# Layer 0 of a four-layer network: one more fold of the bias rows by DMA, another order of the fold's steps on GpSimd, eleven row buffers, and query and value weights of one pair at a time

## The chip, the cores and the metric

The program runs on one core of a Trainium2 chip. The metric is the device time of one execution in microseconds; the kernel before took 3342.97 us (median of three runs, 3342.06 to 3345.39). The engines are TensorE (PE: matmuls; PEld: its weight loads), VectorE (DVE), ScalarE (ACT), GpSimd (POOL) and SyncE (SP, which here only issues DMAs).

## What is computed

Four layers follow each other on an input of 2 x 512 x 32 x 32; only layer 0 is changed. It is a deformable attention with a bias that is computed by a small network. Cut to what matters:

```python
pos  = grid_q[:, :, None, :] - grid_kv[:, None, :, :]   # 1024 queries x 64 keys x 2
bias = sign(pos) * log1p(abs(pos))
bias = relu(bias @ cpb_w1 + cpb_b1)                     # 2 -> 128
bias = relu(bias @ cpb_w2 + cpb_b2)                     # 128 -> 128
bias = bias @ cpb_w3 + cpb_b3                           # 128 -> 1
sim  = einsum('bhid,bhjd->bhij', qh, kh) + bias         # scores
out  = softmax(sim) @ vh
```

There are 2 images and 8 heads, so 16 (image, head) pairs of 1024 queries by 64 keys, and the 2 -> 128 -> 128 -> 1 network is evaluated for each of these million combinations. All of it is in 32-bit floats. Layers 1 to 3 (attention with group norm) and the feed-forward part of layer 0 follow; they are not touched.

## The kernel before, in words

**Tiles and steps.** Two heads make a pair, and a tile is one image and one pair: 8 tiles (`NT`), each of 128 keys on partitions by 1024 queries. The bias of a tile is computed in 32 steps (`NR`) of four keys each; the loop of 256 steps is in `layer0`.

**One step.** `first` (L604, VectorE) adds a row table and a column table and clips at zero: the hidden layer of 128 units for two keys, 1024 queries. Two calls serve a step; they run eight keys ahead, in a ring of six buffers. `second` (L621, PE) multiplies by the 128 x 128 matrix in four parts of 32 units each; in each part the four keys fill the four blocks of 32 partitions of one PSUM tile. ScalarE applies bias and relu (L630) into an SBUF buffer of 128 partitions (4 keys x 32 units) by 1024 queries, 512 KB. The four parts come in the order 1, 0, 3, 2. Parts 1 and 3 go to a pool of four buffers, part 2 to a pool of three, part 0 to a buffer that lives longer.

**Joining and folding.** The last product, 128 -> 1, is a sum over units with signs that were pulled out beforehand. VectorE adds part 1 to part 0 and part 3 to part 2 (`joined`, L635). The rest of the sum over units is done on transfers that add to their destination, which only GpSimd issues:

- the join (L939, 512 KB): the part 2 buffer is added to the part 0 buffer of the same step;
- the first fold (L932, 256 KB): odd partitions are added to even ones;
- the second fold: partitions 2 of 4 are added to partitions 0 of 4 (128 KB), which leaves 32 of the 128 partitions. For the first step of each group of four it is done in place (L934). For the other three, SyncE copies their rows into the group's first buffer (L936, a plain copy) and GpSimd adds the other half there (L942).

So one buffer holds the rows of four steps. `third` (L650, PE) multiplies four such buffers by a matrix of zeros and signs (`w3_16`), four abreast, each 128 x 32 by 512 columns, for two halves of the queries, and so adds 16 steps to `sim` in PSUM. A matmul of this size in 32-bit floats stands in the trace as two records. A tile takes two such calls, 20 steps after the first step of each half. The last 16 steps of the last tile use a shorter form (L921 to L927, L971, and `finish_last`).

**Buffers.** The buffers of group-first steps go round in a ring of six, those of the other steps in a ring of four. Eight of these ten are 4 KB slots per partition of a tile named `bridge` that also carries weights before and sums after the loop.

**Around it.** After the second call of a tile, `scores` adds query times key to `sim`, and a chain of small pieces named `behind` is started: `finish` (softmax and the product with the values), `offsets` of the tile after next, `samples` of the next tile. One piece runs at every odd quarter of a step (k = 1 and 3), so the small work lies spread between the matmuls. `scale_tab` (L592) scales the tables for each four steps on ScalarE, in steps 1 mod 4; SyncE loads them (L573) in steps 2 mod 4.

**What sets the order.** Every engine runs its instructions in the order in which the program text issues them, and each queue, GpSimd's and SyncE's among them, waits in that order: an instruction that waits holds up all behind it. Within a step i and quarter k, before, GpSimd gets: at k = 0 the first fold of step i-2; at k = 1 the join of step i-1, then the second fold of step i-3; at k = 3, for a group's first step only, the second fold of step i-2. SyncE gets the copy of step i-2 at k = 3.

**Weights of layer 0's projections.** Query and value weights stand in block-diagonal form for all four pairs (`bd`, `vwbd`, `qws`); `offsets` uses `qws` of one pair, `samples` the value weights of one pair.

Of the kernel before, what the change touches and what calls it, by code (L numbers as in the profile page):

```python
# [12 lines left out]
F32 = mybir.dt.float32  # L13
# [66 lines left out]
def kernel(ctx: ExitStack, tc: tile.TileContext, a: dict, out: bass.AP):  # L80
# [111 lines left out]
    def layer0(l0, fold_d, t2_b, o2_b):  # L192
# [7 lines left out]
        h2p = cycle([bridge[:, k, :] for k in range(6)])  # L200
        h2j = cycle([bridge[:, 6, :], bridge[:, 7, :], *(one.tile([P, HW], F32, name=f"h2j{k}") for k in range(2))])
# [18 lines left out]
        qkw = next(h2j).rearrange("p (j q n) -> p j q n", j=2, q=NPAIR)  # L220
        vw = one.tile([P, NPAIR, P], F32, name="vwbd")
        bd = {"qw": qkw[:, 0], "kw": qkw[:, 1], "vw": vw}
# [21 lines left out]
        def late_loads():  # L244
            load_groups("vw")
            nc.sync.dma_start(out=xs[1], in_=a["x"][1].rearrange("(k p) n -> p k n", p=P))
# [7 lines left out]
        qws = one.tile([P, NPAIR, P], F32, name="qws")  # L254
        nc.vector.tensor_scalar(qws[:, 0, :], bd["qw"][:, 0, :], s1[:, 0:1], None, ALU.mult)
# [21 lines left out]
        w3_16 = one.tile([P, 48], F32, name="w3_16")  # L277
# [7 lines left out]
        def bias_weights():  # L285
# [5 lines left out]
            few = one.tile([P, 28], F32, name="few")  # L291
# [69 lines left out]
            quarter = few[:, 26:28]  # L361
            for k in range(2):
                nc.vector.tensor_reduce(quarter[:, k : k + 1], ident[:, 2 + k : P : 4], AX.X, ALU.add)
                nc.vector.scalar_tensor_tensor(eighth, quarter[:, k : k + 1], 8.0, eighth, ALU.mult, ALU.add)
            nc.vector.tensor_scalar(w3_16[:, 16:32], row[:, 0:16], eighth, 0.0, ALU.add, ALU.is_equal)
            nc.vector.tensor_scalar(w3_16[:, 16:32], w3_16[:, 16:32], w3sign[:, 1:2], None, ALU.mult)
# [15 lines left out]
        def offsets(t):  # L382
# [4 lines left out]
            for half in range(2):  # L387
                n = slice(half * HALF, (half + 1) * HALF)
                nc.tensor.matmul(pq[:, n], qws[:, pr, :], xs[b][:, pr, n], start=True, stop=True)
# [60 lines left out]
            pos = two.tile([P, 2, 32], F32, name="pos")  # L450
# [14 lines left out]
            sgn = two.tile([P, 2, 32], F32, name="sgn")  # L465
# [19 lines left out]
        def samples(t):  # L485
# [5 lines left out]

            gp = gps.pop(t)
# [7 lines left out]
            near = two.tile([P, 2, 32], F32, name="near")  # L500
            wsum = two.tile([P, 3], F32, name="wsum")
            for ax in range(2):
                nc.scalar.activation(near[:, ax, :], ir, AF.Abs, bias=gp[:, ax : ax + 1], scale=-1.0)
                nc.scalar.activation(
                    near[:, ax, :], near[:, ax, :], AF.Relu, bias=1.0, scale=-1.0, accum_out=wsum[:, ax : ax + 1]
                )
            nc.vector.tensor_mul(wsum[:, 2:3], wsum[:, 0:1], wsum[:, 1:2])
# [33 lines left out]
            nc.tensor.matmul(pkv[:, 1, :], bd["vw"][:, pr, :], kv, start=True, stop=True)  # L541
# [17 lines left out]
        NCH = NR // 4  # L559
        LAST = NT * NR - 16  # L560
        tabs_of = {}

        def load_tabs(c):

            t, rc = divmod(c, NCH)
            assert t in tables
            tabs_of[c] = []
            for ax in range(2):
                src = slog_d[t, ax].rearrange("(q r) i -> q r i", q=4)
                tab = (one if ax else two).tile([P, 16, 32], F32, name=f"tab{ax}")  # L570
                if 4 * c < LAST:
                    q, r = rc % 4, rc // 4 * 16
                    nc.sync.dma_start(out=tab, in_=src[q, r : r + 16, :].partition_broadcast(P))  # L573
                else:
                    q, r = rc % 2 * 2, 16 + (rc - 4) // 2 * 8
                    nc.sync.dma_start(
                        out=tab.rearrange("p (q r) i -> p q r i", q=2),
                        in_=src[q : q + 2, r : r + 8, :].partition_broadcast(P),
                    )
                tabs_of[c].append(tab)  # L580
# [33 lines left out]
        def second(i, h1s, part):  # L614

            z = zt([P, HW], "z")
            lo = BLOCK[part]
            for half in range(2):
                n = slice(half * HALF, (half + 1) * HALF)
                for point in range(4):  # L620
                    nc.tensor.matmul(  # L621
                        z[point * 32 : point * 32 + 32, n],
                        cpb_w2[:, lo : lo + 32],
                        h1s[point][:, half * 16 : half * 16 + 16, :],
                        start=True,
                        stop=True,
                    )
            ring = h2q if part % 2 else h2b if part else h2j if i % (4 if i < LAST else 2) else h2p
            h2 = ring.tile([P, HW], F32, name="h2", tag="h2") if ring in (h2q, h2b) else next(ring)
            nc.scalar.activation(h2, z, AF.Relu, bias=b2h[:, part : part + 1])  # L630
            return h2
# [8 lines left out]
        def third(sim, r, h2s, fours=(), halves=range(2), wide=False):  # L640

            for half in halves:
                n = slice(half * HALF, (half + 1) * HALF)
                w = w3_16[:, 16 - r : 48 - r] if wide else w3[:, 24 - r : 56 - r]
                ways = [(quad, w, h2) for quad, h2 in enumerate(h2s)]
                for k in range(2):
                    w = w3_4[:, 28 - r - 4 * k : 60 - r - 4 * k]
                    ways += [(quad, w, pair[k]) for quad, pair in enumerate(fours, len(h2s))]
                for k, (quad, w, h2) in enumerate(ways):
                    nc.tensor.matmul(  # L650
                        sim[quad * 32 : quad * 32 + 32, n], w, h2[:, n], start=(r == 0 and k < 4), stop=False
                    )
# [9 lines left out]
        def finish(t, sim):  # L662

            b, pr = divmod(t, NPAIR)
            if pr == 0:
                aTs[b] = one.tile([P, NPAIR, HW], F32, name="aT")
            simb = one.tile([P, HW], F32, name="simb", tag="wy")
# [22 lines left out]
            nc.vector.tensor_tensor(atv, atv, sm.unsqueeze(2).to_broadcast([P, 16, NJ]), ALU.mult)  # L690
            yield
# [96 lines left out]
        def key_weights():  # L788
# [26 lines left out]
        nc.vector.tensor_tensor(  # L815
            qws[:, 1:], bd["qw"][:, 1:], s1[:, 1:].unsqueeze(2).to_broadcast([P, NPAIR - 1, P]), ALU.mult
        )
# [3 lines left out]
        nat = [[next(h2p).rearrange("p (k n) -> p k n", k=2) for _ in range(2)] for _ in range(3)]  # L821
# [68 lines left out]
        h1s, parts, joins, sim, w1s = {}, {}, {}, None, None  # L890
        behind = chain(small_steps, offsets(1), samples(0))
# [5 lines left out]
        for i in range(steps):  # L897
            for k, part in enumerate((1, 0, 3, 2)):
# [5 lines left out]
                due = i - 20  # L904
                if k == 1 and 0 <= due < LAST and due % 16 == 0:
                    t, r = divmod(due, NR)
                    if r == 0:
                        sim = ps_s.tile([P, HW], F32, name="sim")
                    third(sim, r, [joins.pop(due + j) for j in range(0, 16, 4)], wide=True)
                    if r:  # L910
                        assert next(behind, None) is None
                        scores(t, sim)
                        behind = chain(
                            finish(t, sim),
                            offsets(t + 2) if t + 2 < NT else iter(()),
                            samples(t + 1) if t + 1 < NT else iter(()),
                        )
# [3 lines left out]
                if LAST <= i - 2 and i < steps - 2:  # L921
# [4 lines left out]
                    if i - 3 >= LAST and i % 2 and k == 3:  # L926
                        nc.gpsimd.dma_start(out=joins[i - 3][1:P:2], in_=joins.pop(i - 2)[1:P:2], accum_op=ALU.add)  # L927
                if 0 <= i - 2 < LAST:
                    j = (i - 2) % 4
                    whole, own = joins[i - 2 - j], joins[i - 2]  # L930
                    if k == 0:
                        nc.gpsimd.dma_start(out=own[0:P:2], in_=own[1:P:2], accum_op=ALU.add)  # L932
                    if k == 3 and j == 0:
                        nc.gpsimd.dma_start(out=own[0:P:4], in_=own[2:P:4], accum_op=ALU.add)  # L934
                    if k == 3 and j:
                        nc.sync.dma_start(out=whole[j:P:4], in_=own[0:P:4])  # L936
# [3 lines left out]
                j = (i - 3) % 4  # L940
                if k == 1 and 0 <= i - 3 < LAST and j:
                    nc.gpsimd.dma_start(  # L942
                        out=joins[i - 3 - j][j:P:4], in_=joins.pop(i - 3)[2:P:4], accum_op=ALU.add
                    )
# [5 lines left out]
                if k == 1 and due == LAST:  # L950
                    third(sim, 16, [joins.pop(due + j) for j in range(0, 8, 2)])
# [1325 lines left out]
```

## Time and profile before

The runs took 3342.97, 3345.39 and 3342.06 us. The profiled execution took 3343.91 us; its span, from the first to the last instruction, is 3342.0 us.

| what | before |
|---|---|
| time of the profiled execution | 3343.91 us |
| its span | 3342.0 us |
| PE busy | 3319.8 us (99%) |
| VectorE busy | 2640.9 us (79%) |
| ScalarE busy | 1809.4 us (54%) |
| GpSimd busy | 675.3 us (20%) |
| loop of layer 0 (first z matmul to the last join's landing) | 57 to 1975 us |
| records of L621 (z) | 16384, 0.59 us each, four abreast |
| records of L650 (sim) | 280 |
| DMA engines busy in the loop | 78 to 79% |

In the profile, a group's line gives the source line, the engine, the operation, the tiles written and read, the count, the busy time and the mean duration in ns, and after the bar the idle time of the engine just ahead of it with what ended that idle time. In a timeline the columns are start and duration in us, engine, line, operation, tiles, and in brackets the idle time before it and what ended it. In a line of the waits stand the engine that waited, for what, and the total in us, the number of waits and the longest. A line of the windows gives the stretch, its length, the busy times of PE, PEld, DVE, ACT and POOL with their counts, the granted clock, the busy share of the DMA engines and GB/s.

### The profile page before, as it was taken

Reading aid. Unit: us, or ns where it says so; the run is one execution under the profiler, and the core shown is the slowest. Engines: PE = TensorE matmul, PEld = TensorE weight load, DVE = VectorE, ACT = ScalarE, POOL = GpSimd, SP = SyncE. Lnnn points to the kernel's source line nnn. Section 1 sums busy time; section 2 is a strip of 40 time slices with the busy share of each in tenths; the row PEclk is TensorE's granted clock in tenths of the full one; section 3 lists DMA queues with packets and bytes.
Section 4 is the critical chain, followed back from the end, with each engine's and each line's share of the span. In section 5 each row is a group of like instructions: output and inputs, shape, how many; then the busy total and the mean of one; then the engine's idle time right before and its main releaser. Section 6 shows DMA issues by size and latency. Waiting matters only on the chain.

```text
span 3342.0 us, 60958 instructions
## 1 busy us (share of the span) xinstructions
PE 3319.8 (99%) x24813; PEld 1605.2 (48%) x24813; DVE 2640.9 (79%) x3029; ACT 1809.4 (54%) x2774; POOL 675.3 (20%) x803
## 2 busy tenths in 40 slices
PE   9999999999999999999999999999999999999999
PEld 4333333333333333333333339999953443687777
DVE  6999999999998799999999966455446465765556
ACT  4866877877876677877867642112126245122221
POOL 1333333333333233333333210000000000000000
PEclk9999999999999999999999999999999999999999
DMA  5777877787787577778877741000100000000111
GB/s 171 158 162 161 162 164 156 158 169 152 160 166 158 107 165 151 161 165 160 166 159 152 161 120 58 14 9 12 51 0 14 26 32 17 7 7 4 29 33 36
DMA packets 142482, 343.91 MB, mean 103 GB/s; under 512 B 36465, under 2 KB 51441, under 8 KB 141425
## 3 DMA queue, kind: packets, MB, share of 16 engines
q0 software_dynamic: 68400, 231.26, 37.1%
q1 hardware_dynamic: 72496, 103.95, 10.1%
q8 instruction: 197, 3.23, 0.4%
q10 hardware_dynamic: 1296, 4.72, 0.4%
q14 instruction: 93, 0.75, 0.1%
HBM read 71.46 MB, written 10.83 MB: 25 GB/s over the span
## 4 chain that ended last, share of the span: by engine, by line
PE 96%; DVE 1%; issue 1%; ACT 1%; DMA 1%; SPq 0%; POOL 0%; DVEq 0%; ACTq 0%; POOLq 0%
PE z L621 52%; PE pma L135 6%; PE pw L1440 6%; PE pmb L135 5%; PE pmv L1440 4%; PE score L1619 3%; PE pv L1631 3%; PE pm L1440 3%; PE score L1440 3%; PE ppr L1440 1%; PE pmt L1440 1%; PE sim L650 1%; PE pf L135 1%; PE pp L710 1%; PE pma L1343 1%
## 5 line engine op out<-in xcount | busy, mean ns | idle before, releaser
L621 PE MATMUL z<-wa,cpb_w 128*32 128x512 f32 x10880 | 1191.9, 593 | 2.7 <-ACT h L630 2.7
L630 ACT ACTIVATE h<-z,b2h 128x1024 f32<-128x1024 f32 x768 | 851.1, 1113 | 331.0 <-PE z L621 301.7
L604 DVE CUSTOM_DVE_ANT_1 wa<-tab,pairs 128x2048 f32<-128x2048 f32 x340 | 776.4, 2284 | 3.1 <-PE z L621 2.6
L621 PEld LDWEIGHTS z<-wa,cpb_w 128*32 128x32 f32 x10880 | 346.5, 110 | 809.3 <-issue 712.4
L621 PE MATMUL z<-h,cpb_w 128*32 128x512 f32 x5504 | 609.5, 593 | 0.7 <-ACT h L630 0.7
L604 DVE CUSTOM_DVE_ANT_1 h<-tab,pairs 128x2048 f32<-128x2048 f32 x172 | 392.7, 2284 | 1.7 <-PE z L621 1.5
L621 PEld LDWEIGHTS z<-h,cpb_w 128*32 128x32 f32 x5504 | 175.1, 110 | 407.9 <-issue 362.7
L635 DVE SCALAR_TENSOR_TENSOR h<-h,turn,h 128x1024 f32<-128x1024 f32 x256 | 327.1, 1278 | 5.5 <-ACT h L630 5.5
L630 ACT ACTIVATE bridge<-z,b2h 128x1024 f32<-128x1024 f32 x162 | 180.8, 1116 | 119.0 <-PE z L621 119.0
L932 POOL DMA_DIRECT2D bridge<-bridge x150 | 127.5, 850 | 539.5 <-DMA bridge<-h 517.5
L635 DVE SCALAR_TENSOR_TENSOR bridge<-bridge,turn,h 128x1024 f32<-128x1024 f32 x162 | 207.0, 1278 | 4.3 <-ACT bridge L630 4.3
L939 POOL DMA_DIRECT2D bridge<-h x161 | 158.4, 984 | 247.0 <-DVE h L635 151.8
L1283 ACT COPY p<-pma 128x128 f32<-128x128 f32 x80 | 21.3, 266 | 334.7 <-PE pma L135 334.7
L1275 DVE TENSOR_TENSOR upper<-pma,p 128x256 f32<-128x256 f32 x80 | 33.7, 421 | 178.6 <-ACT p L1283 178.5
L1620 ACT ACTIVATE p<-score 128x512 f32<-128x512 f32 x256 | 130.0, 624 | 81.2 <-PE score L1619 79.4
L932 POOL DMA_DIRECT2D h2j<-h2j x90 | 76.2, 846 | 314.7 <-DMA h2j<-h 292.6
L630 ACT ACTIVATE h2j<-z,b2h 128x1024 f32<-128x1024 f32 x94 | 104.9, 1116 | 41.5 <-PE z L621 41.5
L1652 DVE TENSOR_TENSOR acc<-acc,p 128x1024 f32<-128x1024 f32 x96 | 111.0, 1217 | 19.5 <-ACT p L1620 19.2
L1619 PE MATMUL score<-q,k 64*128 64x512 f32 x512 | 120.7, 604 | 1.1 <-DVE gm L1196 1.1
L635 DVE SCALAR_TENSOR_TENSOR h2j<-h2j,turn,h 128x1024 f32<-128x1024 f32 x94 | 120.1, 1278 | 0.0
L1631 PE MATMUL pv<-p,vT 128*64 128x512 f32 x512 | 116.5, 598 | 0.0
L942 POOL DMA_DIRECT2D bridge<-bridge x90 | 111.1, 1235 | 0.2 <-issue 0.2
(460 smaller groups left out, 4379.4 us busy)
## 6 DMA issues: line engine op xcount, KB each, us to landing
bridge<-h POOLq DMA_DIRECT2D x161, 512.0 KB, 5.5
h2j<-h POOLq DMA_DIRECT2D x94, 512.0 KB, 5.5
bridge<-bridge POOLq DMA_DIRECT2D x159, 256.0 KB, 3.7
tab<-slog_d SPq DMA_DIRECT2D x128, 256.0 KB, 5.0
h2j<-h2j POOLq DMA_DIRECT2D x90, 256.0 KB, 3.3
bridge<-bridge POOLq DMA_DIRECT2D x150, 128.0 KB, 5.4
bridge<-bridge SPq DMA_DIRECT2D x90, 128.0 KB, 3.6
bridge<-h2j SPq DMA_DIRECT2D x90, 128.0 KB, 3.7
```

What stands on the lines that cost most here:

```text
L135: nc.tensor.matmul(pm, w, m, start=(k == 0), stop=(k == len(pairs) - 1))
L604: nc.vector._custom_dve(TENSOR_ADD_SAT, out=h1, in0=tx.unsqueeze(1).to_broadcast([P, H, 2, W]), in1=ty.unsqueeze(3).to_broadcast([P, H, 2, ...
L621: nc.tensor.matmul(z[point * 32 : point * 32 + 32, n], cpb_w2[:, lo : lo + 32], h1s[point][:, half * 16 : half * 16 + 16, :], start=True, ...
L630: nc.scalar.activation(h2, z, AF.Relu, bias=b2h[:, part : part + 1])
L635: nc.vector.scalar_tensor_tensor(h2, h2, turn[:, part // 2 : part // 2 + 1], parts.pop(part + 1), ALU.mult, ALU.add)
L932: nc.gpsimd.dma_start(out=own[0:P:2], in_=own[1:P:2], accum_op=ALU.add)
L939: nc.gpsimd.dma_start(out=joins[i - 1], in_=other, accum_op=ALU.add)
L942: nc.gpsimd.dma_start(out=joins[i - 3 - j][j:P:4], in_=joins.pop(i - 3)[2:P:4], accum_op=ALU.add)
L1440: nc.tensor.matmul(out, stationary(l, k), moving(r, k), start=start and k == 0, stop=k == nk - 1, skip_group_check=not start,)
L1619: nc.tensor.matmul(sc, ks[m][r, s * P : (s + 1) * P], qs[m][r, n], start=True, stop=True)
L1620: nc.scalar.activation(p[:, part], sc, AF.Exp, scale=64 ** -0.5)
L1631: nc.tensor.matmul(pv[half][part * 64 : part * 64 + 64], vt[s % 4][:, lo : lo + 64], lps[s, half][:, part, :], start=(s == 0), stop=(s == 7),)
```

## The change

**Folds.** For all steps of the first seven tiles and none after (`WIDE` is 224 steps), eight steps share one buffer in place of four. A second fold in place (128 KB, line 969 of the changed kernel) is made for every step; then the fourth fold: for a group's first step in place (64 KB, line 971), for the others a SyncE copy of 64 KB (line 973) into the group's first buffer and a GpSimd addition of 64 KB (line 975). The first half of the last tile goes on sharing among four, with `w3_16`; its last 16 steps have the short form as before.

**Matmuls.** The seven tiles have one call of `third` each, over four buffers of eight steps, with a new sign matrix `w3_32`, at step i-37, k = 3. The call, `scores` and the start of `behind` stand together there; before, the second call stood at step i-20 of the half, k = 1, which is step 36 of the tile. The last tile's call stays at i-20, k = 1. In the built program there are 84 `sim` matmuls of `third` in place of 140.

**Order on GpSimd.** At k = 0 of step i: the second fold of step i-3, and for a group's first step the fourth fold of step i-4; at k = 1: the join of step i-1, then the first fold of step i-2; at k = 2: the addition of step i-4. SyncE copies at k = 3 for step i-3. GpSimd's queue has 971 DMAs in place of 747, SyncE's 671 in place of 615.

**Buffers.** One list of eleven, taken from the front and given back at the end, serves all part 0 results: eight `bridge` slots and three more tiles. Before it were two rings with ten.

**Weights.** `qws` and the new `vws` hold one pair (128 x 128). `samples` loads the value weights, `finish` the query weights for the tile after next, which VectorE scales later in `finish`. `vwbd` is gone. `pos`, `sgn` and `near` have one buffer in place of two, and `samples` has one more piece in the chain.

```diff
-        h2p = cycle([bridge[:, k, :] for k in range(6)])
-        h2j = cycle([bridge[:, 6, :], bridge[:, 7, :], *(one.tile([P, HW], F32, name=f"h2j{k}") for k in range(2))])
+        room = deque([bridge[:, 7, :], *(one.tile([P, HW], F32, name=f"h2j{k}") for k in range(3))])
+        room += [bridge[:, k, :] for k in range(7)]
...
+        def load_group(w, name, pr):
+            for h in range(2):
+                r = slice(h * DH, (h + 1) * DH)
+                nc.sync.dma_start(out=w[r, r], in_=a[name][pr, r, :])
+
+        def scale_queries(pr, src):
+            nc.vector.tensor_scalar(qws, src, s1[:, pr : pr + 1], None, ALU.mult)
...
+        WIDE = (NT - 1) * NR
         LAST = NT * NR - 16
+
+        def shared(i):
+            return 8 if i < WIDE else 4 if i < LAST else 2
...
-            ring = h2q if part % 2 else h2b if part else h2j if i % (4 if i < LAST else 2) else h2p
-            h2 = ring.tile([P, HW], F32, name="h2", tag="h2") if ring in (h2q, h2b) else next(ring)
+            ring = h2q if part % 2 else h2b
+            h2 = ring.tile([P, HW], F32, name="h2", tag="h2") if part else room.popleft()
...
-                due = i - 20
-                if k == 1 and 0 <= due < LAST and due % 16 == 0:
-                    t, r = divmod(due, NR)
-                    if r == 0:
-                        sim = ps_s.tile([P, HW], F32, name="sim")
-                    third(sim, r, [joins.pop(due + j) for j in range(0, 16, 4)], wide=True)
-                    if r:
+                for due, n, turn_of in ((i - 37, 8, 3), (i - 20, 4, 1)):
+                    if k != turn_of or not 0 <= due < LAST or due % NR or shared(due) != n:
+                        continue
+                    t = due // NR
+                    sim = ps_s.tile([P, HW], F32, name="sim")
+                    third(sim, 0, [taken(due + j) for j in range(0, 4 * n, n)], wide=w3_32 if n == 8 else w3_16)
+                    if n == 8:
                         assert next(behind, None) is None
                         scores(t, sim)
                         behind = chain(
...
-                if 0 <= i - 2 < LAST:
-                    j = (i - 2) % 4
-                    whole, own = joins[i - 2 - j], joins[i - 2]
-                    if k == 0:
-                        nc.gpsimd.dma_start(out=own[0:P:2], in_=own[1:P:2], accum_op=ALU.add)
-                    if k == 3 and j == 0:
+                for at in (i - 3, i - 4):
+                    if not 0 <= at < LAST:
+                        continue
+                    n = shared(at)
+                    j, late = at % n, i - 4 - at
+                    own, whole = joins.get(at), joins.get(at - j)
+                    if (k, late) == (0, -1) and (n == 8 or j == 0):
                         nc.gpsimd.dma_start(out=own[0:P:4], in_=own[2:P:4], accum_op=ALU.add)
-                    if k == 3 and j:
-                        nc.sync.dma_start(out=whole[j:P:4], in_=own[0:P:4])
+                    elif (k, late) == (0, 0) and n == 8 and j == 0:
+                        nc.gpsimd.dma_start(out=own[0:P:8], in_=own[4:P:8], accum_op=ALU.add)
+                    if j and (k, late) == ((3, -1) if n == 8 else (0, -1)):
+                        nc.sync.dma_start(out=whole[j:P:n], in_=own[0:P:n])
+                    elif j and (k, late) == ((2, 0) if n == 8 else (3, -1)):
+                        nc.gpsimd.dma_start(out=whole[j:P:n], in_=own[n // 2 : P : n], accum_op=ALU.add)
+                        taken(at)
                 if k == 1 and i - 1 in parts:
                     other = joined(parts.pop(i - 1), 2)
                     nc.gpsimd.dma_start(out=joins[i - 1], in_=other, accum_op=ALU.add)
-                j = (i - 3) % 4
-                if k == 1 and 0 <= i - 3 < LAST and j:
-                    nc.gpsimd.dma_start(
-                        out=joins[i - 3 - j][j:P:4], in_=joins.pop(i - 3)[2:P:4], accum_op=ALU.add
-                    )
+                if k == 1 and 0 <= i - 2 < LAST:
+                    own = joins[i - 2]
+                    nc.gpsimd.dma_start(out=own[0:P:2], in_=own[1:P:2], accum_op=ALU.add)
```

In text, the rest: the code that makes `w3_32` is added to `bias_weights` on VectorE (about ten small operations), and `w3_16` shrinks from 48 to 32 columns.

## The prediction

> **What bounds the kernel now.** I read the page first: the span, the busy times, the chain that ended last. Then the windows for one stretch of the main loop, the chain in order of time around one group of score matmuls, the waits, and GpSimd's timeline, since most of the change lies in its queue.
>
> ```profile
> span 3342.0 us, 60958 instructions
> ...
> PE 3319.8 (99%) x24813; PEld 1605.2 (48%) x24813; DVE 2640.9 (79%) x3029; ACT 1809.4 (54%) x2774; POOL 675.3 (20%) x803
> ...
> PE 96%; DVE 1%; issue 1%; ACT 1%; DMA 1%; SPq 0%; POOL 0%; DVEq 0%; ACTq 0%; POOLq 0%
> ```
> The matrix engine is the end-setting engine nearly everywhere: 96% of the chain. Work taken from it in layer 0 shortens the kernel, if nothing else becomes late.
>
> ```profile
> 440.00:680.00 240.00, 239.33 (x2172) 75.01 (x2168) 231.79 (x151) 182.80 (x254) 85.13 (x100) 1.00 0.78 158
> ```
> One stretch of the loop (length; PE, PEld, DVE, ACT, POOL busy; clock; DMA share; GB/s). PE has 0.7 us idle in 240; VectorE 8.2; the DMA engines are busy 78%. So three resources stand close together.
>
> ```profile
> 1929.61 6.01 PE z L621 x56
> 1935.62 1.72 PE sim L650 x16
> 1937.33 24.08 PE z L621 x224
> ```
> The chain around one call of `third`: 16 matmul records on PE, 1.72 us, nothing beside them on that engine. This is the price of a call.
>
> ```profile
> 664.41 0.86 POOL L932 DMA_DIRECT2D bridge<-bridge  x1 [5.92 <-DMA bridge<-h]
> 664.97 1.19 POOL L939 DMA_DIRECT2D bridge<-h  x1
> 665.51 1.51 POOL L942 DMA_DIRECT2D bridge<-bridge  x1
> 667.93 0.82 POOL L934 DMA_DIRECT2D bridge<-bridge  x1 [0.92 <-DMA bridge<-bridge]
> 670.74 0.85 POOL L932 DMA_DIRECT2D bridge<-bridge  x1 [1.98 <-DMA bridge<-h]
> 671.27 1.22 POOL L939 DMA_DIRECT2D h2j<-h  x1
> ```
> GpSimd's order before: the join of a step (L939), folds of older steps, then the first fold (L932), which waits for its join to land. Where VectorE does not hold it up, join follows join after 671.27 - 664.97 = 6.30 us. A step takes about 7.3, so this chain has a good half microsecond to spare per step. The waits agree:
>
> ```profile
> POOL bridge L932 <- DMA bridge<-h: 517.5, 145, 6.4
> ...
> POOL h2j L932 <- DMA h2j<-h: 292.6, 85, 5.4
> ...
> POOL bridge L939 <- DVE h L635: 151.8, 43, 44.0
> ```
> Every first fold waits for its join, 3.5 us on average; many joins wait for VectorE: there the chain is ahead.
>
> **What the Trainium skill says.** "TensorE: Matmul & The Clock Gate", Part 3 (packing small matmuls): matmuls of different column tiles run together. The trace agrees: 16 records of 592 ns each take 1.72 us, four abreast. "DMA: Bandwidth & Descriptors", Two DMAs through the same engine are not ordered: a DMA that reads what an earlier one wrote must wait for its semaphore, the same queue is no substitute; hence L932's wait. The same page, Issuing engines are not separate DMA queues: SyncE's and GpSimd's transfers interleave on the same 16 engines. Its price (Anatomy of one DMA), 2.0 us plus bytes over 436 GB/s, gives 2.6 us for 256 KB and 3.2 for 512 KB; accumulating transfers here take more: a fold of 256 KB alone lands in 3.2 us, a join of 512 KB alone in 4.6. The measured ones are used: 1.4 us for each further 256 KB, 0.7 for 128 KB, 0.35 for 64 KB.
>
> **The change, part by part.**
> *Matmuls.* A tile of 32 steps had two wide calls of `third` (due 0 and 16); now seven of the eight tiles have one. 15 calls become 8: 7 x 16 = 112 records fewer, 7 x 1.72 = 12.0 us off PE (the 16-record sum at the page's mean rate of 0.44 us for four abreast is 1.76, so 12.3 at most). I take 12.2. All of it lay on the chain. Rows and columns of the rest are the same size.
>
> *VectorE* then has to keep up. Its main-loop work is unchanged. Set against PE's start of each step (end of the step's second L604 against its first z matmul), its first-layer tile was ready 3.4 to 12 us early in nearly every step of before; after 1.72 us less PE work in one place of a tile it should still be 2 us or more early, and where it waits for PE's transposes (6 us a tile, before `mx`) it gives time back. Cost 0; if that lead were gone, up to the whole 12.2. In the preparation some ten tiny operations are added, 0.16 to 0.22 us each: about 2 us, under an idle of 8.26 us that VectorE has before its first first-layer tile (its timeline, the idle in brackets). Cost 0, at most 2.
>
> ```profile
> 50.49 0.16 DVE L860 TENSOR_TENSOR o_b<-pb,pc 128x4 f32<-128x4 f32 x1 [8.26 <-PE pb L135]
> ```
>
> *Weights of one pair.* Per tile two SyncE loads of value weights and two of query weights (32 KB or less per pair of issues, about 0.6 us of SyncE's queue each) and one small VectorE scaling. In `finish` the load stands nine turns ahead of the scaling, some 30 us against landings of 5 to 7; the first such load waits only for the first `pq` matmul, at 13 us, and is needed at 25.6. The value weights have ten turns. SyncE mostly waits for folds, so a few issues ahead of a copy delay nothing that is due. One 0.46 us memset goes from GpSimd's start, where SyncE's issues are the later ones. Cost 0; a microsecond or two if a load is late.
>
> *ScalarE.* The finishing work of a tile starts three half-steps later, so its extra activations fall on other parts of the loop. Its lead over PE's buffer reuse is 2 us mostly and 0.3 us at its worst, once a tile, for several alignments of before. A collision may cost up to 1 us a tile; I take 1.5 us in all, between 0 and 7.
>
> *GpSimd's queue* is the open term. It gets 971 DMAs in place of 747, four per step. The order is now join of the newest step, first fold of the one before, fourth fold (64 KB), second fold (128 KB), next join. The second fold waits for the first fold, which is queued directly behind a 512 KB join. One turn, from landing to landing of the first fold: 0.28 us until GpSimd goes on (L932 after a join's landing), second fold issued, 0.55 us later the join (as 664.41 to 664.97), which lands 4.8 us on (5.5 behind a 256 KB fold, less 0.7 for the smaller transfer ahead), the first fold 1.4 us after that. Sum 7.03, against the same sum for before of 0.28 + 0.55 + 5.5 = 6.33 (measured 6.30). The chain gets 0.70 longer per step. Table loads come every fourth step. Where GpSimd was behind for four steps of before, the starts of L939 in its timeline give the pitch with loads: 293.80 to 320.66 is 26.9, and three other places have 25.5, 26.8 and 27.4; the mean is 6.65 a step. Adding 0.70 gives 7.35. The low end, where loads fall into the queue's idle 2 us of each turn, is 7.2; the high end, with a SyncE copy of 0.17 always in the way and the fold of a group's first tile (0.05), 7.55.
> The loop's step after the change: by the starts of its first z matmuls, steps 0 to 223 took 1675.9 us (57.4 to 1733.2), less 28 for one long projection stage and 12 saved: 7.30. At 7.35 the chain falls behind by 0.05 x 224 = 11 us. The eleven buffers take that up: the tightest reuse in a tile is 1.75 steps (12.8 us) after the fold that frees it is issued; with queueing some 5 us remain, and 2 more by ScalarE's lead: 7 us, once before and once after the long stage, which resets the lag: 14. So cost 0 at 7.35, and (pitch - 7.30) x 224 - 14 above 7.36: 42 us at 7.55. Below nothing is excluded: the chain off the bound gives PE nothing.
>
> Sum against the profiled execution: 3343.9 (span 3342.0 and 1.9 around it) - 12.2 + 1.5 = 3333.2. The median of the runs is 0.9 below the profiled one: 3332.3; I give 3333.
>
> **Rivals.**
> *The lag eats the gain.* Pitch 7.39 to 7.44: 10 us of stalls at 7.41, 3341. For it: the sum's error is as large as the margin. Against it: long steps at each tile's start, up to 12 us between joins, in which the chain catches up.
> *GpSimd's DMA chain becomes the bound*, slower. At 7.55 per step it loses 56 us over 224 steps, 14 absorbed: 3343 - 12 + 42 = 3373. It decides from 7.45 on (14 + 12.2 + 6.7 over 224). Place: ScalarE waits for a buffer of the first-part tiles, PE for ScalarE. For it: DMA at 78%, and the dependent fold behind the largest transfer. Against it: the four-step sums.
> *Another cover is too thin*: ScalarE or VectorE fall late at the new alignment, 3 us a tile, 3355. Against: no alignment of before did that.
> That the matmuls are not removed is excluded: the built program has 56 calls of 512 columns fewer, two records each.
>
> **How the numbers follow.** Forecast 0.47, lag within measurement 0.17, chain bound 0.31, other cover 0.05. What a measurement can tell from no change is about 0.2%, 6.7 us: faster 0.47, same 0.17, slower 0.36. The range starts at 3329.5 (12.3 saved, no stall, 1 us of scatter) and goes to 3369, which leaves out the worst of the chain case. The forecast's own range is 3329.5 to 3336.
>
> **What would show it.** Right: L621's groups unchanged, `sim` records 280 down to 168, PE's idle in the windows still under 1 us in 240, GpSimd's joins about 7.3 apart with some waits for VectorE left. Wrong: ScalarE's activation of first-part tiles waiting for a DMA, PE's z matmuls waiting for ScalarE, joins 7.45 apart or more and none of them waiting for VectorE; or, with the chain idle, waits of PE for VectorE.

## The result, and the profile after

The changed kernel took **3538.32 us** (median of five runs, 3533.70 to 3547.93), the kernel before 3342.97 us beside it (five runs, 3342.06 to 3346.13). The ratio is 1.0585 with a 95% interval of 1.0573 to 1.0597: 195 us slower. The prediction was 3333 us, with a range up to 3369.

The profiled execution took 3533.7 us. The page of the changed kernel, at the places that were shown of before:

```profile
span 3531.8 us, 61269 instructions
...
PE 3368.5 (95%) x24701; PEld 1597.7 (45%) x24701; DVE 2651.8 (75%) x3045; ACT 1806.3 (51%) x2774; POOL 861.9 (24%) x1028
...
PE 50%; DMA 30%; issue 8%; POOL 8%; DVE 3%; ACT 1%; POOLq 0%; SPq 0%; DVEq 0%; ACTq 0%
```

PE has 112 records fewer, as intended, but it is no longer the engine that sets the end everywhere: its share of the chain went from 96% to 50%, and transfers, the issue times between them and GpSimd took 46%. The work behind the loop of layer 0, where PE still leads, is 39% of the span; so within the loop the chain is mostly GpSimd and its transfers. The windows, the same stretch as before:

```profile
440.00:680.00 240.00, 222.92 (x1948) 66.66 (x1944) 213.00 (x140) 163.14 (x226) 99.46 (x117) 0.97 0.79 150
```

PE has 17 us idle in 240, in place of 0.7, at a granted clock of 0.97 in place of 1.00. The waits tell who is behind whom:

```profile
POOL bridge L969 <- DMA bridge<-bridge: 694.4, 149, 6.5
...
POOL h2j L969 <- DMA h2j<-h2j: 341.3, 70, 6.4
...
ACT h L656 <- DMA bridge<-h: 139.8, 55, 5.4
POOL bridge L979 <- DVE h L661: 97.3, 14, 45.2
...
PE z L647 <- ACT h L656: 64.0, 59, 3.9
```

Nearly every second fold (L969; 219 of 228) waits for its first fold, 4.7 to 4.9 us on average; ScalarE waits for buffers whose folds have not landed; PE waits for ScalarE. Joins into `bridge` that wait for VectorE were 43 (L939); 14 are left (L979). The prediction named these as the signs of its rival. One turn in GpSimd's timeline:

```profile
717.28 0.84 POOL L969 DMA_DIRECT2D bridge<-bridge  x1 [4.72 <-DMA bridge<-bridge]
717.82 1.19 POOL L979 DMA_DIRECT2D bridge<-h  x1
718.36 1.53 POOL L982 DMA_DIRECT2D bridge<-bridge  x1
718.90 1.78 POOL L975 DMA_DIRECT2D bridge<-h2j  x1
725.21 0.84 POOL L969 DMA_DIRECT2D bridge<-bridge  x1 [4.53 <-DMA bridge<-bridge]
```

The second fold, the join, the first fold and the fourth fold's addition are issued within 1.6 us; then GpSimd stands still until the first fold, queued behind the join, has landed. And the chain in order of time, in the same place, is nothing but this:

```profile
717.28 0.84 POOL bridge L969
718.12 0.07 POOL bridge L979
718.18 0.18 issue
718.36 6.57 DMA bridge<-bridge
724.93 0.28 issue
725.21 0.84 POOL bridge L969
```

Read from one second fold to the next, the turn is 7.93 us here. PE needs 7.34 for a step, by the tiles of 235.0 us (32 steps) of run 6 below, where GpSimd does not hold it up.

Where the 190 us of span lie, from the starts of the z matmuls in the traces:

| us | first z matmul | tiles 0 to 6 | tile 7 | rest |
|---|---|---|---|---|
| before | 57.4 | 1675.9 | 235.0 | 1373.8 |
| after | 64.3 | 1849.7 | 245.2 | 1372.6 |

So 174 us in the seven tiles with the fourth fold, 10 in the last tile (which begins with the lag of the others), 7 ahead of the loop, nothing behind it.

The theory from this: GpSimd's turn, two landings in series, became longer than PE's step. Rivals: the 16 DMA engines' throughput is the limit, whatever the order; or SyncE's copies or loads hold the folds up; or the weights' loads do.

### The profile page after: what moved, and what is told of

It reads as the page before. It is cut to its first block, busy times and chain, and to the rows that moved or that the text cites. A ratio compares the mean times of both kernels' runs of the same rounds, so it can differ in the third digit from the quotient of the medians.

```text
span 3531.8 us, 61269 instructions
## 1 busy us (share of the span) xinstructions
PE 3368.5 (95%) x24701; PEld 1597.7 (45%) x24701; DVE 2651.8 (75%) x3045; ACT 1806.3 (51%) x2774; POOL 861.9 (24%) x1028
## 4 chain that ended last, share of the span: by engine, by line
PE 50%; DMA 30%; issue 8%; POOL 8%; DVE 3%; ACT 1%; POOLq 0%; SPq 0%; DVEq 0%; ACTq 0%
DMA bridge<-bridge 19%; PE z L647 10%; DMA h2j<-h2j 9%; PE pma L135 6%; PE pw L1478 5%; PE pmb L135 5%; PE pmv L1478 4%; PE score L1657 3%; PE pv L1669 3%; POOL bridge L969 3%; PE pm L1478 3%; PE score L1478 3%; PE pp L740 1%; POOL h2j L969 1%; PE ppr L1478 1%
## 5 line engine op out<-in xcount | busy, mean ns | idle before, releaser
L647 PE MATMUL z<-wa,cpb_w 128*32 128x512 f32 x10880 | 1210.6, 597 | 55.7 <-ACT h L656 46.1
L647 PEld LDWEIGHTS z<-wa,cpb_w 128*32 128x32 f32 x10880 | 339.2, 110 | 888.0 <-issue 694.5
L647 PE MATMUL z<-h,cpb_w 128*32 128x512 f32 x5504 | 624.8, 602 | 20.0 <-ACT h L656 17.9
L969 POOL DMA_DIRECT2D bridge<-bridge x157 | 131.5, 838 | 731.0 <-DMA bridge<-bridge 694.4
L982 POOL DMA_DIRECT2D bridge<-bridge x164 | 250.2, 1526 | 3.4 <-issue 2.0
L661 DVE SCALAR_TENSOR_TENSOR bridge<-bridge,turn,h 128x1024 f32<-128x1024 f32 x176 | 226.2, 1285 | 9.4 <-ACT bridge L656 9.3
L656 ACT ACTIVATE bridge<-z,b2h 128x1024 f32<-128x1024 f32 x176 | 196.5, 1117 | 70.0 <-PE z L647 62.1
L979 POOL DMA_DIRECT2D bridge<-h x175 | 206.9, 1182 | 100.7 <-DVE h L661 97.3
L975 POOL DMA_DIRECT2D bridge<-bridge x106 | 177.4, 1673 | 26.7 <-DMA bridge<-bridge 26.4
L969 POOL DMA_DIRECT2D h2j<-h2j x71 | 59.4, 836 | 346.9 <-DMA h2j<-h2j 341.3
L982 POOL DMA_DIRECT2D h2j<-h2j x76 | 114.1, 1501 | 0.0
```

The costliest lines, as they stand in the source:

```text
L647: nc.tensor.matmul(z[point * 32 : point * 32 + 32, n], cpb_w2[:, lo : lo + 32], h1s[point][:, half * 16 : half * 16 + 16, :], start=True, ...
L661: nc.vector.scalar_tensor_tensor(h2, h2, turn[:, part // 2 : part // 2 + 1], parts.pop(part + 1), ALU.mult, ALU.add)
L975: nc.gpsimd.dma_start(out=whole[j:P:n], in_=own[n // 2 : P : n], accum_op=ALU.add)
L979: nc.gpsimd.dma_start(out=joins[i - 1], in_=other, accum_op=ALU.add)
```

## Experiments

All times are medians; ratios are to the kernel before, run beside them, with 95% intervals. The "turn" is the time from join to join, averaged over the steps 31 to 221 in which the join is issued over 0.7 us after VectorE had it ready (late joins).

**1. The order of before, with all else of the change.** GpSimd's order in a step: first fold (waits for the join), join, addition, second fold. SyncE's copies move with it, one step earlier.

```diff
-                    if (k, late) == (0, -1) and (n == 8 or j == 0):
-                        nc.gpsimd.dma_start(out=own[0:P:4], in_=own[2:P:4], accum_op=ALU.add)
...
+                    if k == 0:
+                        nc.gpsimd.dma_start(out=own[0:P:2], in_=own[1:P:2], accum_op=ALU.add)
+                    if k == 2 and (n == 8 or j == 0):
+                        nc.gpsimd.dma_start(out=own[0:P:4], in_=own[2:P:4], accum_op=ALU.add)
...
```

> The changed kernel with one thing undone: GpSimd's order. Per step it now issues first fold, join, the addition of a group's fourth fold, second fold, so that the first fold again stands ahead of the next join and the second fold lies behind the join. Transfers, buffers, matmuls are those of the changed kernel. Theory A (the time went because the second fold waits for a first fold that is queued behind a 512 KB join): the pitch of the joins falls from 8.3 us to 6.3 to 6.8, PE sets the time again, 3331 to 3345 us. Rival B (too many transfers for GpSimd and the DMA engines, 971 in place of 747, in any order): stays above 3480 us.

Measured: 3369.68 us, 1.0079 (1.0065 to 1.0093). Neither range is met, but 169 of the 195 us are gone: the order makes the most of the loss. What remains is some 10 us ahead of the loop and 17 in the tiles. The turn is 7.49 in its mean, just above PE's step. It has one landing in it: joins land 6.61 us after their issue, and 0.28 + 0.55 make it 7.44.

**2. The new order alone, on the kernel before** (four steps to a buffer, old buffers and weights).

```diff
-                    if k == 0:
-                        nc.gpsimd.dma_start(out=own[0:P:2], in_=own[1:P:2], accum_op=ALU.add)
...
+                if k == 1 and 0 <= i - 2 < LAST:
+                    own = joins[i - 2]
+                    nc.gpsimd.dma_start(out=own[0:P:2], in_=own[1:P:2], accum_op=ALU.add)
...
```

> The kernel before with the new order alone: join of the newest step ahead of the first fold of the step before; four steps share a buffer, as before. Only one step in four has a second fold on GpSimd that depends on the first fold just ahead of it. Theory A: that step gets a pitch near 8, the others under 6.5, mean near 6.8, so PE still sets the time: 3343 us, within 10. Rival C (a fold queued behind a join is dear in every step, whatever waits for it): 3400 us or more.

Measured: 3354.98 us, 1.0037 (1.0023 to 1.0050), between the two, near the first. So the order does most of its harm together with the fourth fold, which needs a second fold in every step. Here only one step in four has one on GpSimd: of the 41 late joins, 31 come right after such a second fold, with a turn of 8.58 us on the mean, near theory A's 8. Most of the others still go as soon as VectorE is ready (58% of all joins within half a microsecond of it), so the chain catches up. GpSimd also has three DMAs a step here in place of four; this run does not part the two.

**3. Without SyncE's copies.**

```diff
-                    if j and (k, late) == ((3, -1) if n == 8 else (0, -1)):
+                    if j and n == 4 and (k, late) == (0, -1):
                         nc.sync.dma_start(out=whole[j:P:n], in_=own[0:P:n])
```

> The changed kernel without SyncE's copies of 64 KB into the shared buffer in the first seven tiles (the upper half of the folded rows of seven steps in eight is left out of the sum; the additions stay). The first fold takes 2.2 us from the join's landing to its own where a copy's packets fall into it, 1.7 where none do, and I had put down 1.4. Theory A1 (the copies add the 0.5 to 0.8 us a step that my sum lacked): pitch 7.4 to 7.7, time 3370 to 3430 us. Rival A2 (a copy of 16 packets costs its 0.17 us and the rest comes from elsewhere): 3490 us or more.

Measured: 3506.11 us, 1.0481 (1.0465 to 1.0497). Rival A2, in its time and its size: the copies cost 32 us of 195, and the turn is 8.08 in place of 8.24.

**4. The weights of one pair alone, on the kernel before.**

```diff
-        qws = one.tile([P, NPAIR, P], F32, name="qws")
+        qws, vws = [one.tile([P, P], F32, name=n) for n in ("qws", "vws")]
...
```

> The kernel before with the weights of one pair at a time alone (loads of query and value weights per tile, one small scaling each, no buffer for all pairs). Theory A: hidden, 3343 us within 3. Rival D (SyncE's extra issues delay copies or tables): slower by 7 us or more.

Measured: 3352.18 us, 1.0025 (1.0014 to 1.0036): 8 us slower, all of it ahead of the loop. The seven tiles take 1675.8 us, as before, and the first z matmul starts at 65.3 in place of 57.4. So neither theory's place was right: the loop's loads cost nothing, the start does.

**5. Without the table loads.** The tables are loaded once.

```diff
+            tabs_of[c] = [held, held] if held is not None else []
+            for ax in range(0 if held is not None else 2):
...
```

> The changed kernel with the tables of the first layer loaded once: the later 63 pairs of 256 KB loads by SyncE are left out and every step's tables are scaled from the first tile's second table, so the first-layer values, and with them the output, are not the reference's. ScalarE's scalings and all of VectorE's and GpSimd's work stay. Theory A (GpSimd's turn is set by landings, and a step's share of table loads costs 0.7 us of it: 8.24 us less 0.7 is 7.5, against the 7.37 that PE needs): tiles of 266 us fall to 241 to 246, 3538 to between 3350 and 3410. Rival B (the order alone holds the turn at 8 whatever SyncE moves): tiles stay above 258 us, time above 3470. My prediction's own term, 0.35 a step, would give 7.9 a step, tiles of 253 us, about 3440.

Measured: 3508.38 us, 1.0491 (1.0474 to 1.0509); turn 8.12. The time is in rival B's range. Theory A of this run falls: after run 3 I had put 0.7 us a step on the loads, and they give back 0.12.

**6. One DMA moved.** The second fold is issued one place later, behind the next join.

```diff
-                    if (k, late) == (0, -1) and (n == 8 or j == 0):
-                        nc.gpsimd.dma_start(out=own[0:P:4], in_=own[2:P:4], accum_op=ALU.add)
...
                     nc.gpsimd.dma_start(out=joins[i - 1], in_=other, accum_op=ALU.add)
+                at = i - 3
+                if k == 1 and 0 <= at < LAST and (shared(at) == 8 or at % shared(at) == 0):
+                    nc.gpsimd.dma_start(out=joins[at][0:P:4], in_=joins[at][2:P:4], accum_op=ALU.add)
```

> The changed kernel with one thing moved: a tile's second fold is issued behind the next join in GpSimd's queue instead of ahead of it, so the wait for the first fold's landing no longer stands before a join, and the queue holds a join while GpSimd waits. Same transfers, same buffers, all of the sum computed. Theory A (the turn is a chain of landings: join, first fold, then the next join's issue): the chain is broken, joins go at PE's pace of 7.4 us, tiles of 236 to 240 us, time 3340 to 3365 with the start-up's 7 to 10 us still in it. Rival B (the 16 DMA engines' throughput is the limit, with 960 KB of accumulating transfers and 64 KB of copies per step): the turn stays at 8 us or more, time above 3490.

Measured: **3344.72 us**, 1.0003 (0.9995 to 1.0012). Theory A, and fully: the same transfers, 194 us faster. Five of the seven tiles take 235.0 to 235.1 us, in place of 236.3 to 236.5 before; the first takes 228.1, the one with the long projection stage 263.7 (before: 229.7 and 264.4). GpSimd's timeline of this run (L977 the join, L980 the second fold, L983 the first fold, L973 the addition):

```profile
733.58 0.78 POOL L973 DMA_DIRECT2D h2j<-bridge  x1 [1.79 <-DMA h2j<-bridge]
734.46 0.90 POOL L977 DMA_DIRECT2D bridge<-h  x1
737.22 0.81 POOL L980 DMA_DIRECT2D h2j<-h2j  x1 [1.86 <-DMA h2j<-h2j]
737.74 1.18 POOL L983 DMA_DIRECT2D bridge<-bridge  x1
740.68 0.78 POOL L973 DMA_DIRECT2D h2j<-bridge  x1 [1.77 <-DMA h2j<-bridge]
```

GpSimd still waits for landings, but for transfers issued 5 to 7 us earlier, while a join or a first fold behind them is already being moved. Its waits show that the chain is off the bound:

```profile
POOL bridge L977 <- DVE h L661: 495.0, 126, 45.0
...
POOL bridge L980 <- DMA bridge<-bridge: 66.1, 52, 3.3
```

Joins wait for VectorE again, 126 of them into `bridge` in place of 14. The same stretch as before:

```profile
440.00:680.00 240.00, 239.34 (x2166) 74.20 (x2162) 233.82 (x153) 183.80 (x255) 112.54 (x133) 1.00 0.85 165
```

PE is idle for 0.7 us in 240 again. The kernel moves 165 GB/s with the DMA engines 85% busy, the changed kernel 150 and 79%: throughput was not the limit.

**7. The first load of one pair's query weights by GpSimd**, on the kernel of run 4.

```diff
-        load_group(qws, "qw", 1)
+        load_group(qws, "qw", 1, nc.gpsimd)
```

> The kernel before with the one-pair weights, with the first load of one pair's query weights issued by GpSimd instead of SyncE. Theory A (the 7 to 10 us later start comes from ScalarE's last weight load, which waits for a semaphore that the first, 768 KB, load shares once SyncE's two small loads stand between them in the count; qpad is queued behind it): qpad starts at 13 us as in the kernel before instead of 19, first z matmul at 57 to 58 us instead of 65, time 3342 to 3346. Rival B (the load itself comes late for its matmul): the start stays at 64 to 65 us, time 3350 to 3354.

Measured: 3344.78 us, 1.0004 (0.9995 to 1.0012): theory A. ScalarE's queue in the changed kernel:

```profile
9.58 8.41 ACTq L119 DMA_DIRECT2D wa<-in_proj_w  x4
18.12 1.15 ACT L408 ACTIVATE qpad<-pq,qb 128x1024 f32<-128x1024 f32 x1 [15.87 <-DMA wa<-in_qkv_w]
```

and in this run:

```profile
10.07 2.08 ACTq L119 DMA_DIRECT2D wa<-in_proj_w  x4
13.47 1.15 ACT L400 ACTIVATE qpad<-pq,qb 128x1024 f32<-128x1024 f32 x1 [11.23 <-PE pq L398]
```

In the traces, the DMAs of ScalarE and SyncE in the first 30 us use eight completion semaphores again and again, one set for both engines. In the kernel before and in this run, ScalarE's last four weight loads, the L119 line above, reuse semaphores that are free by then, and start at about half a microsecond from each other. In the changed kernel SyncE's two small loads take two places of the round, and the third of ScalarE's four gets the semaphore of SyncE's 1536 KB load of the input, issued at 7.88 us. That one lands at 17.15, and the third load starts at 17.17, where the second had started at 10.15. (The expectation had the right kind of wait, but the last load and a 768 KB one.) `qpad` stands behind these loads on ScalarE, and all of `offsets` behind `qpad`. The profile's bracket at `qpad` names an earlier weight load; the starts of the DMAs tell the wait.

**8. Both edits (6 and 7) on the changed kernel.**

> The changed kernel with both edits: the second fold issued behind the next join, and the first load of one pair's query weights by GpSimd. All of the sum is computed. Theory A: 7 to 8 us below the run with the second fold alone, so 3332 to 3357, and below the kernel before if the tiles keep 236 us or less. Rival B: as with the second fold alone, above 3480.

Measured: **3336.61 us** (3334.01 to 3338.36, 12 runs), against 3343.35 of the kernel before (31 runs): 0.9980 (0.9971 to 0.9989). This is theory A, 8 us below run 6, and this version beats both kernels, the one before by 0.2%. Its span is 9.8 us below that of before: seven tiles 9.0 shorter, start 0.7 earlier, rest 1.6 shorter, last tile 1.5 longer.

**9 to 11. What lengthens the turn in the order of the change.** Run 9 leaves out the fourth fold's additions, run 10 the copies and the table loads, run 11 all three.

```diff
                     elif j and (k, late) == ((2, 0) if n == 8 else (3, -1)):
-                        nc.gpsimd.dma_start(out=whole[j:P:n], in_=own[n // 2 : P : n], accum_op=ALU.add)
+                        if n == 4:
+                            nc.gpsimd.dma_start(out=whole[j:P:n], in_=own[n // 2 : P : n], accum_op=ALU.add)
```

> The changed kernel, its order kept, without GpSimd's 64 KB addition of a tile's folded rows to the first tile of its group (seven of eight steps of the first seven tiles of the feature maps): half of those rows are left out of the sum. SyncE's copies and the table loads stay. In the changed kernel GpSimd's turn is 8.24 us on the mean over the steps in which it is late: join's landing 5.31 after its issue, first fold's landing 1.99 after that, 0.31 to the second fold's issue, 0.63 to the next join. Theory A (the addition's packets mix into the first fold ahead of it, and lie ahead of the next join): fold 1.6 to 1.8 after the join, join 5.0, turn 7.5 to 7.8, time 3370 to 3440. Rival B (it lies behind both and costs nothing): turn 8.1 or more, time above 3500.

> The changed kernel without SyncE's 64 KB copies in the first seven tiles (a quarter to a half of the folded rows is left out) and with the tables loaded once (as in the run without tables): SyncE has almost no transfers in the loop. Singly the two gave back 32 and 30 of 195 us. Theory A (both only lengthen single landings; the turn without them is 0.28 + 0.55 + 4.9 + 1.65 = 7.38, at PE's own step of 7.37): time 3350 to 3400, turn 7.4 to 7.6. Rival B (their effects do not add, the turn is held by GpSimd's own transfers and their order): turn 7.8 or more, time above 3450.

> The changed kernel without copies, tables after the first, and the addition, as in the two runs beside it: GpSimd's queue has the join, the first fold and the second fold alone, in the order of the change, and all else of the sum is left out. This is the bare turn of my prediction: 0.28 + 0.55 + 4.8 + 1.4 = 7.03. Theory A (that bare sum holds): joins wait for VectorE, tiles of 235 to 237 us, time 3336 to 3350. Rival B (the first fold takes 1.65 or more behind the join even so): turn above 7.3 and tiles of 238 us or more, time above 3355.

In the table, "join's landing" is from the join's issue, and each further column starts where the one to its left ends; the four add up to the turn. All times are in us.

| kernel | time | ratio (interval) | turn | join's landing | first fold after it | to second fold | to join |
|---|---|---|---|---|---|---|---|
| after | 3538.3 | 1.0585 (1.0573 to 1.0597) | 8.24 | 5.31 | 1.99 | 0.31 | 0.63 |
| 3, no copies | 3506.1 | 1.0481 (1.0465 to 1.0497) | 8.08 | 5.32 | 1.82 | 0.31 | 0.63 |
| 5, no tables | 3508.4 | 1.0491 (1.0474 to 1.0509) | 8.12 | 5.20 | 1.98 | 0.31 | 0.63 |
| 9, no additions | 3490.2 | 1.0440 (1.0420 to 1.0461) | 8.08 | 5.20 | 1.94 | 0.29 | 0.64 |
| 10, no copies, no tables | 3457.5 | 1.0345 (1.0325 to 1.0366) | 7.87 | 5.20 | 1.73 | 0.31 | 0.63 |
| 11, none of three | 3386.7 | 1.0131 (1.0111 to 1.0151) | 7.56 | 5.12 | 1.51 | 0.30 | 0.64 |

Run 9 lies between its theories, nearer the rival; runs 10 and 11 took the rival's times, though run 11's first fold, 1.51 us behind the join, is below the 1.65 that its rival named. None of the three causes carries the loss alone, and even with all three gone the mean turn is above PE's step. GpSimd's timeline of run 11 (L973 the second fold, L984 the join, L987 the first fold) shows one reason:

```profile
581.06 0.83 POOL L973 DMA_DIRECT2D h2j<-h2j  x1 [4.85 <-DMA h2j<-h2j]
581.60 1.18 POOL L984 DMA_DIRECT2D bridge<-h  x1
582.14 1.55 POOL L987 DMA_DIRECT2D bridge<-bridge  x1
588.06 0.84 POOL L973 DMA_DIRECT2D bridge<-bridge  x1 [4.37 <-DMA bridge<-bridge]
```

This turn is 7.00 us. The one from 557.50 to 565.92 is 8.42, with the same transfers. What differs stands in the DMA queues of the stretch from 558 to 566 us:

```profile
q8 instruction: 1, 0.02, 0.7%
```

One packet of 16384 bytes, which held one DMA engine for 0.95 us while the join was being moved. The Trainium skill, "Runtime: NRT & Kernel Launch", section Instruction fetch mechanics, says that a sequencer refills its instructions in 16 KiB blocks over a DMA queue of its own, and that the cost is mostly hidden. The trace agrees on the size (each of the 196 packets on that queue in run 11 has 16384 bytes), but turns with such a packet are longer: of run 11's late turns, the 96 in which none began between a join's issue and the landing of the first fold behind it took 7.18 us on the mean (7.01 the median), the 85 with one 7.99. In the changed kernel, where other transfers already stretch the landings, it is 8.11 against 8.43. This is a coincidence in time that is seen in every one of these runs, not an experiment: no run was without these packets. A longer turn also has more room for a packet. With the times of all packets shifted together, by 4 to 60 us either way, run 11's difference of 0.81 us becomes 0.11 on the mean and 0.71 at most. So the packets may cause much of it; that is not shown.

## Why the prediction was wrong, point by point

**Matmuls: right.** The 12.2 us went off PE: `sim` records of `third` 280 to 168, a call still 1.72 us. The chain of the changed kernel shows it in a place where PE leads:

```profile
2100.00 26.62 PE z L647 x250
2126.62 1.72 PE sim L676 x16
2128.34 24.08 PE z L647 x224
```

In run 8, where GpSimd's chain is off the bound, 9.0 us of them came out over the seven tiles: a tile takes 1.3 us less (235.0 in place of 236.3), where a call costs 1.72. A call in run 8 has 12 semaphore waits ahead of it in PE's queue of weight loads, 0.11 us apart, where one of before has four; whether these are the missing 0.4 was not tested.

**VectorE: right.** The first-layer tile stayed ahead of PE; run 6 reached 235 us tiles with VectorE's work unchanged. At the start it begins later, but behind `qpad`, not for its own work:

```profile
57.46 0.16 DVE L889 TENSOR_TENSOR o_b<-pb,pc 128x4 f32<-128x4 f32 x1 [7.98 <-PE pb L135]
```

It stood at 50.49 before, with nearly the same idle time, 8.26.

**Weights: "cost 0; a microsecond or two if a load is late" was wrong by 7 us.** The working compared a load with its consumer. The load was not late (its edit in run 7 moves nothing but the queue, and the first z matmul starts at 57.6 us again, in place of 65.3). What it cost was its place in the round of semaphores, by the traces: it made another engine's DMA wait, with an activation queued behind.

**ScalarE: 1.5 us, between 0 and 7, was not separated.** The loop of run 8 is 7.5 us shorter where 12.2 went off PE. The remainder of 4.7 holds the 0.4 us of each of seven tiles and 1.5 us in the last tile; how much of it is ScalarE's stays open.

**GpSimd's queue: here the prediction failed**, at "Adding 0.70 gives 7.35". The two landings in series were in its sum; what it mis-sized is the term for what shares the engines with them. The bare sum 0.28 + 0.55 + 4.8 + 1.4 = 7.03 holds for undisturbed turns: those of run 11 without an instruction packet have a median of 7.01, with 4.90 for the join, 1.27 for the fold, and 0.28 and 0.54 for the issues (so the errors of join and fold cancel in part). The term on top of it was 0.32 us, carried over from four-step sums of before (6.65 against the sum of 6.33), and measured it is 1.21: joins land after 5.31 us in place of 4.8, first folds 1.99 later in place of 1.4, and the issues take 0.94 in place of 0.83.

By the ladder of runs: 7.01 bare; 7.18 the mean of turns with no instruction packet; 7.56 with them; 7.87 with the additions (run 10); 8.24 with copies and table loads as well. The step from 7.18 to 7.56 goes with the packets and is not shown to be theirs; the later ones are by experiment. The sum had no term for the addition; 0.31 us is what run 10 has more than run 11. In the order of before, GpSimd waits for one landing in most turns, the join's; a late first fold delays a second fold in one step of four, and otherwise only buffers. In the new order the turn holds two landings in series, and a delay of either one adds to the turn, at every step.

The rival's own formula, with the measured turn, then gives the result: (8.24 - 7.30) x 224 - 14 = 197; 3343.9 - 12.2 + 1.5 + 197 + 7 for the start = 3537, against 3533.7 of the profiled execution. The step of 7.30 in it was right: run 8's seven tiles give 7.32 by the same working, (1666.9 - 28) / 224. So the mechanism was on the list, with its place and its chain of waits (GpSimd, ScalarE, PE), but "the range 7.2 to 7.55" did not hold the turn, and the range of times ended with it. From the forecast's 7.35 to the 7.45 from which the rival decides there was 0.10 us a step, less than any single one of the terms that the runs took apart (copies alone 0.16, table loads alone 0.12, additions 0.16 alone and 0.31 last).

**The DMA share as evidence.** The prediction listed "DMA at 78%" for the rival. It was no evidence: run 6 ran at 85% without loss. Landings in a dependent chain bound the changed kernel, not the engines' capacity.

## What to carry to other kernels

When the order in an in-order queue is changed, count the landings that stand in series between one issue of an instruction and its next. Here copies, table loads and additions each lengthened such a turn, and an allowance measured with one landing in the turn was too small for two. A DMA that waits for one just issued belongs behind the next independent DMA in the queue, not ahead of it: one place later was worth 194 us here. A new DMA also takes a place in the round of completion semaphores, and the DMA that pays can be another engine's (here 7 to 9 us at the start).

## What the runs showed of the hardware

- Where PE stood idle more, its granted clock was lower. The changed kernel has 112 records fewer, but PE's busy time rose from 3319.8 to 3368.5 us, and the mean granted clock fell from 0.998 to 0.983. In the second tile the z matmuls kept PE busy for 231.3 us in place of 222.1, beside 19 us of idle time. Of the 16384 z records 220 took longer than the 617 ns that is the longest of before, up to 1063. With one DMA moved (run 6) the clock is 0.998 again and no z record is longer than 617 ns. So on PE the loss shows in part as slower work and not as idle time; what sets the time is still GpSimd's turn.
- A 16 KB instruction packet takes 1.07 us on the mean (0.98 the median) in the loop of the changed kernel, and there is one for about every second step (100 in 190). In run 11, the join with one beside it in the turn from 557.50 landed after 6.37 us, the one without in the turn from 581.06 after 4.94.
- With SyncE's copies of 64 KB, 16 packets of 4096 bytes each, the first fold landed 1.99 us after the join, without them 1.82; the join's own landing, 5.31 and 5.32, did not move.
